# Weighing before copying: the order of two readers of one PSUM bank in a four-layer network

## The chip, the cores and the metric

The kernel is one launch on one core of a Trainium2 chip. The metric is the device time of a whole execution in microseconds; lower is better. All arithmetic is in float32.

## The reference, cut to what matters

The input is 4 images of 32 x 32 tokens with 384 channels. Four residual layers follow each other; the change lies in layer 1, an attention with 12 heads of width 32 whose weights are multiplied by a "group weight":

```python
sim = sigmoid(beta + alpha * einsum('bhnd,bhmd->bhnm', l2norm(xg_h), l2norm(gc)))   # n = 1024, m = 256
group_weight = einsum('bhnm,bhkm->bhnk', sim, sim)                                   # n x n, symmetric
gamma = sigmoid(group_gamma)
group_weight = group_weight * gamma + (1.0 - gamma)
attn = softmax(einsum('bhnd,bhmd->bhnm', q, k) * scale, axis=-1)
attn = attn * group_weight
attn = attn / (attn.sum(axis=2, keepdims=True) + 1e-08)
out = einsum('bhnm,bhmd->bhnd', attn, v)
```

Layer 0 is a deformable attention with a gathered bias, layer 2 a box filter, layer 3 an outlook attention; they are untouched.

## The kernel before

The four images are worked in two lanes. The *front* computes layer 0 of an image; the *trunk* computes layers 1 to 3. While the trunk works on image b, the front's generator is advanced for image b + 1, so that both lanes' instructions are recorded interleaved; for the last image the trunk is alone. A scheduler then puts each engine's instructions in an order by priorities and by its own estimates, places the tiles and sets the semaphores. So a change in one place of the source can move instructions of either lane on every engine, and the order is fixed when the program is built.

Layer 1 works in six *pairs* of heads (`pair`, p = 0 to 5). In a pair, r = 0, 1 names the head. The 1024 x 1024 matrices are worked in eight steps j = 0 to 7 of 128 rows, and each step in two halves h = 0, 1 of 512 columns. A step does this:

- L1443: GpSimd scales the step's 128 columns of `sim` into `sg` (by gamma and a constant).
- L1460: TensorE makes the logits of both heads in a two-bank tile `big`, with 64 rows of the array for each head; L1468: ScalarE takes the exponential into `e`. A tile `big` exists twice.
- For each half h and head r, TensorE makes 128 x 512 group weights in one PSUM bank `ps`. The matrix is symmetric: blocks already computed in an earlier step are transposed from a kept copy (L1485), the others are made by matmuls of `sg` and `sim` (L1490).
- L1498: where the bank holds blocks that a later step needs, ScalarE copies them to `keep` (tiles `gn` and `gf`; 1 to 4 blocks of 128 columns). This is so for 480 of the 768 banks.
- L1499: VectorE *weighs*: it adds 1 - gamma to the bank, multiplies by `e` in place, and leaves the row sums in `tot`.
- After the halves of h = 0, `sums_step` prepares the next pair's softmax sums: L1333 makes logits (four matmuls, on 32 rows of the array each) in two `big` tiles, L1341 (VectorE) takes their maximum and L1342 (ScalarE) the exponential in place, with its sum.
- `values` of the step before: L1423 to L1426 (VectorE) make reciprocal sums and scale the values, and L1432 (TensorE) multiplies them with `e` into the bank `av`.

In step 6 `sums_finish` turns the next pair's sums into logarithms by small operations (L1359 to L1365 on VectorE, L1362 on ScalarE), L1367 transposes them on TensorE, L1370 stores them and `load_lse` (L1309) loads them as an additional row of the queries; L1303 loads queries and keys. In the last step `sims` (L1380, L1388, L1391) computes the next pair's `sim`.

There are four single PSUM banks (`bank`) in rotation for everything, one of them taken by `av` through a pair. The front takes its own from the same four: L820 (attention logits), L833 (transposes of a running maximum, made by L826 on VectorE), L841 (broadcast by a matmul, after L839 on GpSimd), L855 (attention values). The front's other operations named later are L799 (gathers, GpSimd's queue), L811 and L816 (ScalarE) and L812 and L817 (VectorE), which interpolate the bias, and L853 (ScalarE's exponential).

Two readers of one bank never overlap: the semaphores let them follow each other as the source has them. Where there is a copy, the weighing of L1499 waits for it, and TensorE may write the bank again after both.

## Time and profile before

| What | us |
|---|---|
| Median of 3 runs | 4660.67 (4658.08 to 4672.65) |
| The profiled execution | 4698.26, span 4696.5 |
| TensorE busy in the span | 4148.5 |
| VectorE busy | 3181.2 |
| ScalarE busy | 2293.4 |
| GpSimd busy | 948.8 |
| L1499, weighing: 768 of 749 ns | 562.4 |
| L1498, copies: 192 of 583 ns (`gf`); 96 each of 475, 369 and 263 ns (`gn`) | 106.3; 45.1, 35.4 and 25.2 |
| L1490, group weights on TensorE | 865.1 |

PE is TensorE, PEld its weight loads, DVE VectorE, ACT ScalarE, POOL GpSimd and SP the queue that issues most DMAs. Busy times overlap and do not add up to the span. In a list of waits, "A <- B: t, n, m" says that A's engine sat idle for t us in all, n times, at most m us, until B was done. In the timeline a bracket gives the idle time ahead of an instruction and what ended it.

### The profile page before, as it was taken

The numbers are of one execution on the slowest core, as the hardware profiler recorded it, in microseconds if no ns is written. First come the engines' busy times: TensorE is split into PE (matmuls) and PEld (weight loads), VectorE is DVE, ScalarE is ACT, GpSimd is POOL, SyncE is SP. The second block draws the span as 40 slices with busy tenths as digits, with TensorE's granted clock in tenths as the row PEclk, the third lists the DMA queues.
The fourth block names the chain that finished last, engine by engine and source line by source line (L and its number), as shares of the span: only waits on it lengthen the run. The fifth ranks groups of instructions, "written<-read, shape, count | busy, mean of one in ns | idle before, by whom it ended". The sixth has DMA issues, their size and how long they took to land. (4 is left out here: it accounts for less than half of the span.)

```text
span 4696.5 us, 46832 instructions
## 1 busy us (share of the span) xinstructions
PE 4148.5 (88%) x15704; PEld 1782.4 (38%) x15704; DVE 3181.2 (68%) x6005; ACT 2293.4 (49%) x3631; POOL 948.8 (20%) x946
## 2 busy tenths in 40 slices
PE   5477797999999988999999989899999998999998
PEld 2222243333333353433333444333333345343444
DVE  3599755787868726677877763768787884565654
ACT  2166433566656313456665432446565651455532
POOL 0533204221212103311211110422021211000000
PEclk8688898999999988999999989899999998999998
DMA  6435234322212144321211124531121213311011
GB/s 124 132 112 152 65 103 131 90 62 55 71 33 70 58 139 131 114 62 51 82 51 56 58 79 116 161 91 53 37 78 51 75 37 115 108 31 27 19 40 41
DMA packets 232819, 370.98 MB, mean 79 GB/s; under 512 B 117732, under 2 KB 165697, under 8 KB 232577
## 3 DMA queue, kind: packets, MB, share of 16 engines
q1 hardware_dynamic: 171560, 201.49, 14.7%
q0 software_dynamic: 39936, 145.53, 10.6%
q10 hardware_dynamic: 21080, 20.96, 1.8%
q8 instruction: 124, 2.03, 0.2%
q14 instruction: 119, 0.97, 0.1%
HBM read 287.90 MB, written 80.27 MB: 78 GB/s over the span
## 5 line engine op out<-in xcount | busy, mean ns | idle before, releaser
L1490 PE MATMUL bank<-whole,sg 128*128 128x512 f32 (+3 forms) x2304 | 865.1, 510 | 8.3 <-POOL sg L1443 6.9
L1499 DVE SCALAR_TENSOR_TENSOR e<-bank,gam,e 128x512 f32<-128x512 f32 x768 | 562.4, 749 | 445.9 <-ACT gn L1498 159.6
L1342 ACT ACTIVATE big<-big,nmax 128x1024 f32<-128x1024 f32 x384 | 418.5, 1090 | 353.5 <-DVE nmax L1341 338.0
L1468 ACT ACTIVATE e<-big 128x1024 f32<-128x1024 f32 x384 | 379.5, 1018 | 412.2 <-PE big L1460 406.3
L1490 PEld LDWEIGHTS bank<-whole,sg 128*128 128x128 f32 x2304 | 407.4, 199 | 376.6 <-issue 286.5
L1341 DVE TENSOR_REDUCE nmax<-big 128x1 f32<-128x1024 f32 x384 | 454.8, 1220 | 70.0 <-PE big L1333 38.7
L799 POOL DMA_INDIRECT win<-strips,widx x288 | 311.5, 1082 | 683.8 <-DVE z L812 408.9
L1443 POOL TENSOR_SCALAR sg<-whole,gam 128x512 f32<-128x512 f32 x192 | 150.3, 785 | 1453.1 <-PE bank L1490 1003.6
L1460 PE MATMUL big<-qa,ka 64*128 64x512 f32 x1536 | 422.4, 622 | 8.2 <-ACT big L1342 7.6
L1333 PE MATMUL big<-k,q 32*128 32x512 f32 x1536 | 328.3, 679 | 77.9 <-ACT e L1468 40.7
L820 PE MATMUL bank<-qpad,kz 128*128 128x512 f32 x576 | 281.8, 617 | 12.4 <-DVE e L1499 12.4
L714 POOL DMA_INDIRECT gat<-pairs,sidx x192 | 206.3, 1075 | 410.9 <-DVE ix_gt L500 223.6
L855 PE MATMUL bank<-lg,va 128*64 128x512 f32 x576 | 266.0, 606 | 15.0 <-ACT lg L853 14.9
L855 PE MATMUL bank<-lg,ones 128*64 128x512 f32 x576 | 265.3, 605 | 0.0
L817 DVE SCALAR_TENSOR_TENSOR lg<-z,bias_f,lg 128x512 f32<-128x512 f32 x288 | 221.1, 776 | 40.2 <-ACT lg L816 39.0
L811 ACT ACTIVATE z<-win,bias_f 128x528 f32<-128x528 f32 x288 | 208.4, 738 | 66.7 <-DVE lg L817 32.3
L1460 PEld LDWEIGHTS big<-qa,ka 64*128 64x128 f32 x1536 | 138.0, 186 | 263.1 <-issue 155.6
L812 DVE SCALAR_TENSOR_TENSOR z<-win,bias_f,z 128x528 f32<-128x528 f32 x288 | 214.6, 763 | 26.3 <-DMA win<-strips,widx 16.8
L852 DVE TENSOR_TENSOR lg<-lg,tb 128x512 f32<-128x512 f32 x288 | 187.4, 697 | 42.4 <-ACT tb L845 42.4
L1432 PE MATMUL bank<-e,vs 128*32 128x512 f32 x1536 | 206.7, 604 | 1.0 <-DVE vs L1426 1.0
L816 ACT ACTIVATE lg<-z,bias_f 128x512 f32<-128x512 f32 x288 | 200.3, 718 | 13.6 <-PE bank L855 6.7
L821 DVE TENSOR_TENSOR lg<-bank,lg 128x512 f32<-128x512 f32 x288 | 192.2, 685 | 20.2 <-PE bank L820 18.3
(302 smaller groups left out, 6593.9 us busy)
## 6 DMA issues: line engine op xcount, KB each, us to landing
pairs<-xn SPq DMA_DIRECT2D x64, 192.0 KB
q<-qd SPq DMA_DIRECT2D x48, 256.0 KB
w<-in_gmat SPq DMA_DIRECT2D x16, 576.0 KB
w<-in_w_off SPq DMA_DIRECT2D x12, 576.0 KB
w<-in_Wqkv SPq DMA_DIRECT2D x12, 576.0 KB
a<-in_x SPq DMA_DIRECT2D x16, 384.0 KB
x<-a ACTq DMA_DIRECT2D x4, 1536.0 KB
win<-strips,widx POOLq DMA_INDIRECT x384
```

Of the source, the lines that this page charges most:

```text
L799: nc.gpsimd.indirect_dma_start(out=win, out_offset=None, in_=self.strips[:, :], in_offset=bass.IndirectOffsetOnAxis(ap=self.widx[:, q, c : ...
L812: v.scalar_tensor_tensor(z, wv[:, 1 : HH + 1, 0 : HW + 1], sc(0, 1), z, ALU.mult, ALU.add)
L817: v.scalar_tensor_tensor(lg, z[:, :, 1 : HW + 1], sc(0, 0), lg, ALU.mult, ALU.add)
L820: nc.tensor.matmul(ps, kz[:, j * P : (j + 1) * P], both, start=True, stop=True)
L855: nc.tensor.matmul(po[out, :], w, lf, start=j == 0, stop=j == NJ - 1)
L1333: nc.tensor.matmul(ps[r][:, h * 512 : (h + 1) * 512], self.q4[rows, i * P : (i + 1) * P], self.k4[rows, 0:512], start=True, stop=True,)
L1341: v.tensor_reduce(nmax[:, r, i : i + 1], ps[r], AX.X, ALU.max, negate=True)
L1342: nc.scalar.activation(ps[r], ps[r], AF.Exp, bias=nmax[:, r, i : i + 1], accum_out=den[:, r, i : i + 1],)
L1460: nc.tensor.matmul(ps[:, r, :], ka[rows, j * P : (j + 1) * P], qa[rows, cols], start=True, stop=True,)
L1468: nc.scalar.activation(e, ps, AF.Exp)
L1490: nc.tensor.matmul(ps[:, (mid - i0) * P :], sg[:, r, m, :], sim[:, h, r, m, (mid - i0) * P :], start=m == 0, stop=m == 1,)
L1499: v.scalar_tensor_tensor(e[:, r, :], ps, self.gam[:, 1:2], e[:, r, :], ALU.add, ALU.mult, accum_out=tot[:, r, h : h + 1],)
```

## The change

In the loop over the heads r of `pair`, the weighing now stands ahead of the copy in the source. Both read the same bank, so their semaphores turn round: the weighing waits for TensorE, and the copy waits for the weighing. Nothing else is edited. In the changed kernel the weighing is L1497 and the copy L1502.

```diff
                                 start=m == 0,
                                 stop=m == 1,
                             )
-                    if first < i1:
-                        nc.scalar.copy(keep[:, r, :], ps[:, (first - i0) * P :])
                     v.scalar_tensor_tensor(
                         e[:, r, :], ps, self.gam[:, 1:2], e[:, r, :], ALU.add, ALU.mult,
                         accum_out=tot[:, r, h : h + 1],
                     )
+                    if first < i1:
+                        nc.scalar.copy(keep[:, r, :], ps[:, (first - i0) * P :])
```

The scheduler builds another order from this: compared as lists of instructions, the two orders differ in 108 lines of TensorE's 8898 (removed and added ones counted), 806 of VectorE's 5239, 634 of ScalarE's 3325, 68 of SP's 998 and 20 of GpSimd's 951.

## The prediction

> **What bounds the kernel now.** I read the page first, then the busy time by stretch, then the waits of TensorE and VectorE, then the chain of waits and the timeline at the places that these name. The page:

> ```profile
> PE 4148.5 (88%) x15704; PEld 1782.4 (38%) x15704; DVE 3181.2 (68%) x6005; ACT 2293.4 (49%) x3631; POOL 948.8 (20%) x946
> ```

> TensorE has most of the span. The edited instructions live in layer 1's pairs, which run in four stretches: three in which the next image's front shares the engines (784 to 1600, 1990 to 2700, 3090 to 3800 us) and the last image alone (4066 to 4560 us). Busy time in the third and the last (columns: stretch, length, then PE, PEld, DVE, ACT, POOL in us with counts, granted clock, DMA share, GB/s):

> ```profile
> 3090.00:3800.00 710.00, 662.21 (x2621) 268.96 (x2620) 554.04 (x1092) 430.69 (x692) 147.83 (x152) 0.98 0.23 65
> 4066.00:4560.00 494.00, 480.43 (x2131) 207.74 (x2129) 287.67 (x675) 265.19 (x419) 33.96 (x50) 0.99 0.11 28
> ```

> In a shared stretch TensorE idles 710 - 662 = 48 us and VectorE is 78% busy; alone, TensorE idles 14 us of 494. The first two shared stretches leave 53 and 46 us. All idle TensorE time that the edit could touch is thus about 147 + 14 = 161 us, 3.4% of the span. VectorE's largest waits on ScalarE, whole run:

> ```profile
> DVE e L1499 <- ACT gn L1498: 159.6, 163, 4.0
> DVE e L1499 <- ACT gf L1498: 157.9, 101, 2.0
> ```

> Weighings (L1499) stood idle for 317.5 us until the copy (L1498) of the same bank was done. That is the wait which the edit removes; but it is VectorE's, and counts only where TensorE then waits. TensorE's waits in the third stretch:

> ```profile
> PE big L1333 <- ACT e L1468: 13.7, 14, 1.8
> PE bank L1367 <- DVE dsum L1365: 5.5, 5, 1.4
> PE bank L841 <- POOL diag L839: 5.1, 6, 1.0
> PE bank L833 <- DVE rmax L826: 4.6, 7, 1.7
> PE bank L820 <- DVE e L1499: 4.1, 4, 1.6
> PE big L1333 <- ACT big L1342: 4.0, 4, 1.5
> PE bank L855 <- ACT lg L853: 2.4, 3, 1.0
> PE bank L1485 <- DVE e L1499: 2.3, 2, 1.4
> PE big L1380 <- ACT e L1468: 1.8, 2, 1.0
> ```

> VectorE ended 5.5 + 4.6 + 4.1 + 2.3 = 16.5 us, ScalarE 13.7 + 4.0 + 2.4 + 1.8 = 21.9 us. The first sum can shrink, the second can grow.

> [...] a copy starts at 4177.70 and takes 0.27, its weighing starts at 4178.00. [...] in the chain eight 64-row matmuls of L1460, issued together, take 1.92 us, and two that a matmul of L1367 had cut off take 1.73:

> ```profile
> 4174.51 1.92 PE big L1460 x8
> 4221.81 1.73 PE big L1460 x2
> ```

> **The change part by part.** No instruction, byte or DMA is added or removed.

> *The wait removed.* All 480 weighings whose bank is also copied waited for ScalarE. In the changed program they wait for TensorE alone (and for the exponentials, long done). I lined up the 120 copies of the stretch 3000 to 3800 us with their weighings, each put at the later of its bank's last matmul and the end of the VectorE instruction that stands ahead of it in the changed order: 93 start earlier, by 79 us together; in the last image 100 of 120, by 85 us.

> *The wait added.* Each copy now waits for its weighing (749 ns, and 84 ns for the accumulator's read), and behind it in ScalarE's queue wait exponentials and front work. By the same count 51 of 120 copies hold up the next ScalarE instruction, 36 us in that stretch (mostly L853, L811, L816). ScalarE had 710 - 431 = 279 us idle there; its share of the chain of waits in that stretch was 90 of 679 us, 13%. I price the hold-up at that share: 36 x 0.13 = 4.7 us a stretch. From both sides: nothing, if the scheduler's new order hides it, or a third of it (12 us), if it lands on exponentials for which TensorE waits.

> *The order moved.* The scheduler reacts: L1342's second exponential often goes ahead of the first copy, and weighings go ahead of front work (L812, L817) on VectorE. On TensorE 11 of L1460's groups that were split 3 + 1 come together (29 to 18), L1380 loses one split an image, L1333 gains two an image. At 1.73 - 0.96 = 0.77 us a split (0.96 is half of 1.92), a shared stretch gains 2 + 1 - 2 = 1 of them, 0.8 us; the price for the other two lines is unknown and taken as the same (0 to 1.5). On SP's queue the store of lse and its two reloads (L1370, L1309) pass two loads of qa and ka (L1303), which are needed a pair later; on POOL three operations an image trade places with gathers issued many blocks ahead. Both cost nothing while that distance covers them[...].

> *Last image, each pair but the last, at the end of its sums.* The timeline now:

> ```profile
> 4217.52 0.26 ACT L1498 COPY gn<-bank 128x128 f32<-128x128 f32 x1
> 4218.92 0.18 DVE L1359 CAST dsum<-den 128x16 f32<-128x16 int32 x1 [0.35 <-ACT big L1342]
> 4219.07 0.75 DVE L1499 SCALAR_TENSOR_TENSOR e<-bank,gam,e 128x512 f32<-128x512 f32 x1
> 4219.75 0.17 DVE L1360 TENSOR_SCALAR dsum<-dsum 128x16 f32<-128x16 f32 x1
> 4221.53 0.28 PE L1367 MATMUL bank<-ident,dsum 128*16 128x128 f32 x1 [1.27 <-DVE dsum L1365]
> ```

> The second weighing sits inside the chain from L1359 to L1367. In the changed order both weighings run ahead of L1359, at 4217.45 to 4218.9, while ScalarE does its exponentials; L1359 starts as before, three tiny operations take the weighing's place, and two copies (0.26 each) stand before L1362. L1360 ends near 4219.3 in place of 4219.92; I take 0.55 us. L1367 now stands ahead of both matmuls of the second L1460 tile, which saves the split, 0.77. Together 1.3 us for each of 5 pairs: 6.6 us. At a pair's first step the copy (0.49) leaves the path to L1341, but L1333 ends only 0.16 us ahead of it: 0.2 x 5 = 1 us. The other steps gain nothing, TensorE having no gap there. Last image: -7.6 us.

> *A shared stretch.* L1367: 5 x 0.55 = 2.75 us. L833: VectorE is late since two weighings waited behind two exponentials and a copy (3243.8 in place of 3242.1 us); 1.7 us is more than the 0.66 us of each wait, and it is the cause in about 5 of 7: 3 us. L1485: about half, 1 us. L820: nothing, since a bank comes free when both readers are done, whichever is last. Splits 0.8. Sum 7.5, less 4.7: 2.8 us, three times: 8.4 us.

> Total -7.6 - 8.4 = -16 us. The profiled execution took 4698.26 us (span 4696.5), 0.8% over the median of 4660.67, so it would read 4682; the median, 4660.67 - 16 = about 4645 us.

> **The rivals.**
> (a) *VectorE was the late one* (chance 0.20): the whole 16.5 us a stretch goes, as do the diag waits (5.1) behind L833: 3 x 21.6 + 7.6 = 72 us, 4590 us. For it: 79 us of earlier starts on an engine 78% busy. Against: TensorE then meets ScalarE's 21.9 us.
> (b) *The hold-up passes to ScalarE and decides* (0.30): copies sit at the head of ScalarE's queue in the shared stretches until a VectorE with 78% of its time taken serves them, exponentials L1468 come late, and L1333, which waits for their tile (13.7 us already), waits longer. At a third of 36 us with the gains of 7.5 halved: 3 x (12 - 3.8) - 7.6 = +17 us, 4678; with all gains gone, 4689. It decides once more than 7.5 + 2.5 = 10 of the 36 us, 28%, reach TensorE.
> (c) *Nothing in the shared stretches* (0.18): the two waits cancel and only the last image gains: 4653 us, within the noise.
> My forecast itself has 0.32. That the edit does nothing is excluded: the built program shows all 480 waits turned round.

> **How the numbers follow.** A measurement of this kernel can tell about 0.3% (14 us) from no change. Forecast: more than half of the outcomes near -16 are beyond it, so of 0.32 I put 0.23 to faster; (a) adds 0.20: 0.43. Within 0.3%: 0.09 of the forecast, 0.16 of (c), 0.02 of (b): 0.27. Slower: 0.28 of (b), 0.02 of (c): 0.30. The range runs from 4600, most of (a), to 4690, (b) with all gains gone; the forecast's own range is 4630 to 4657.

> **What would show it.** In the changed profile VectorE's waits on copies should be gone, with copies waiting on weighings in their place, some 100 us or more in all. In the last image L1460's second tile should end 1.3 us sooner after L1333 in each pair's step 6 (the wait of L1367 by itself need not shrink, as L1367 now stands a matmul earlier), and the pairs 7 to 8 us sooner. L833's wait should fall from 4.6 to under 2 us a stretch. L1333's wait for L1468 should stay under 18 us a stretch; if it passes 25, (b) is right. Were the last image not shorter, my reading of L1367 would be wrong.

## The result and the profile after

The changed kernel is faster: 4635.8 us median against 4660.67 us in the first measurement, a ratio of 0.9945 (95% interval 0.9928 to 0.9962), 25 us (18 to 34). Two repetitions, e1_after and e3_after below, gave 0.9942 (0.992 to 0.9965) and 0.9918 (0.99 to 0.9937). The profiled execution took 4633.41 us (span 4631.6).

The page after, and the busy time by stretch, in a shared stretch and in the last image (columns as in the prediction; the windows lie where the same work now stands):

```profile
PE 4107.5 (89%) x15704; PEld 1772.9 (38%) x15704; DVE 3182.5 (69%) x6005; ACT 2310.3 (50%) x3631; POOL 948.7 (20%) x946
```

```profile
3035.00:3745.00 710.00, 664.69 (x2623) 270.37 (x2622) 556.70 (x1092) 436.25 (x692) 147.03 (x150) 0.97 0.22 66
4015.00:4496.00 481.00, 470.11 (x2129) 204.57 (x2129) 286.35 (x674) 267.09 (x419) 33.55 (x50) 1.00 0.11 28
```

VectorE's and ScalarE's work is what it was. TensorE now idles 710 - 664.7 = 45 us in the shared stretch (48 before) and 11 us in the last image (14). The last image's window holds the same 2129 to 2131 matmuls in 481 us instead of 494; some 3 us of that difference is clock, by my estimate. The clock records hold only 1.0 and 0.5, in multiples of 3.41 us (see below); I call each 3.41 us a window. Four windows of this stretch were halved in the first profile and one after. In the profiles of the two repetitions e1_before and e1_after none was, and the five pairs take 409.5 and 400.7 us. The first profile's take 414.0, 4.5 us more than e1_before's; shared among its four halved windows this is 1.1 us each, and the estimate is three of them. The waits of VectorE and ScalarE, whole run:

```profile
DVE e L1497 <- PE bank L1490: 219.5, 224, 3.8
...
ACT gn L1502 <- DVE e L1497: 132.4, 121, 4.1
...
DVE e L1497 <- PE bank L1485: 122.7, 51, 5.6
```

The 317.5 us that weighings stood idle for copies are gone, but VectorE's idle time ahead of the weighings falls by less, from 445.9 to 346.0 us in all, since most of it is now a wait for TensorE. Copies now wait for weighings: 132.4 us here and 48.8 for gf, 181 us together. TensorE's waits in the shared stretch (3039 to 3749 us):

```profile
PE big L1333 <- ACT e L1468: 11.2, 10, 2.0
PE bank L1367 <- DVE dsum L1365: 5.6, 5, 1.5
PE big L1333 <- ACT big L1342: 5.0, 5, 1.5
PE bank L833 <- DVE rmax L826: 3.3, 6, 1.8
PE bank L820 <- ACT gf L1502: 3.1, 2, 1.6
PE big L1380 <- ACT e L1468: 2.8, 2, 1.5
PE bank L841 <- POOL diag L839: 2.7, 3, 1.0
PE big L1460 <- ACT big L1342: 2.5, 1, 2.5
...
PE bank L841 <- DMA gc<-gcd: 1.7, 2, 0.8
```

L1333's wait for the exponentials L1468, the place where rival (b) had to show, is 11.2 us instead of 13.7. L820 now waits for a copy where it waited for a weighing, for 3.1 us instead of 4.1. L1367's wait is unchanged. L841's wait for diag is 2.7 us instead of 5.1, but a row of 1.7 us that names a DMA stands beside it now, so that L841 waits 4.4 us in all.

Where the time went shows at two places of each pair. The chain of waits in the last image, end of a pair's sums; before (columns: start, length, what):

```profile
4300.89 1.22 DVE nmax L1341
...
4304.69 0.18 DVE dsum L1359
4304.86 0.74 DVE e L1499 x2
4305.60 0.09 DVE dsum L1360
...
4307.29 0.28 PE bank L1367
4307.57 1.05 PE big L1460 x2
```

and after:

```profile
4239.83 0.24 PE big L1333 x3
...
4242.41 1.42 DVE e L1497 x4
4243.83 0.17 DVE dsum L1359
...
4244.21 0.08 DVE rt L1424
...
4245.81 0.28 PE bank L1367
4246.09 1.06 PE big L1460 x4
```

In this view one weighing is x2, as its record is followed by that of the accumulator's read (0.08 us). The second weighing has left the stretch between L1359 and L1367; both now stand ahead of L1359. The stretch takes 4307.29 - 4304.69 = 2.60 us before, 4245.81 - 4243.83 = 1.98 after. From the end of L1333 to the start of L1367 it is 6.40 us before and 5.74 after. Now a pair's first step, before:

```profile
4157.51 1.09 ACT big L1342
...
4158.64 1.20 ACT big L1342 x2
4159.85 0.48 ACT gf L1498
...
4160.35 0.76 DVE e L1499 x2
4161.11 1.15 DVE nmax L1341
...
4162.35 1.21 ACT big L1342 x2
...
4163.60 1.82 PE big L1460 x5
```

and after:

```profile
4183.55 1.21 ACT big L1342 x2
...
4184.81 1.13 PE big L1333 x4
...
4185.94 1.13 PE big L1333 x4
4187.06 1.91 PE bank L1490 x4
4188.98 1.48 PE big L1460 x5
```

Before, the chain ran through the copy, the weighing, the maximum and the exponentials, and TensorE waited at L1460; from the first L1342 to L1460 it took 6.09 us. After, copy and weighing are off the chain, TensorE's own matmuls are the chain, and it takes 5.43.

**A yardstick free of the clock.** The medians of the kernel before lay between 4660.67 and 4695.83 us in four sessions (the last three on three different chips), and its two profiles have granted clocks of 0.927 and 0.933. The clock records hold only 1.0 and 0.5 (full and half clock), in pieces that are multiples of 3.41 us (but for the last piece, which the record's end cuts): 170 pieces in the first profile before, 146 in the one after. So I took, in each profile, the time from an image's first L1460 to the first L1460 of its sixth pair, times the mean granted clock in it. In the three profiles whose shared stretches are as before this "full-clock length" is 625.9, 626.0 and 625.8 us (mean of three images), in three of the changed kernel 619.4, 620.0 and 619.4. In e1_shared, whose shared stretches have the changed kernel's orders too, it is 617.9. The last image: 407.2 and 409.5 before, 400.6, 400.7 and 400.5 after. The product takes 3.41 x 0.5 = 1.7 us off for a halved window even where TensorE stood idle in part of it: I take this to be why the first profile, with four halved windows there, comes to 407.2 and e1_before, with none, to 409.5. So I read these lengths to about 2 us. The edit is worth some 6.4 us in each shared stretch and some 8 in the last image (8.8 between the two profiles without a halved window): 3 x 6.4 + 8 = 27 us, what the chip's times say.

### The profile page after: what moved, and what is told of

It reads as the page before. It is cut to its first block, busy times and chain, and to the rows that moved or that the text cites. A ratio compares the mean times of both kernels' runs of the same rounds, so it can differ in the third digit from the quotient of the medians.

```text
span 4631.6 us, 46942 instructions
## 1 busy us (share of the span) xinstructions
PE 4107.5 (89%) x15704; PEld 1772.9 (38%) x15704; DVE 3182.5 (69%) x6005; ACT 2310.3 (50%) x3631; POOL 948.7 (20%) x946
## 4 chain that ended last, share of the span: by engine, by line
PE 59%; DVE 19%; ACT 7%; issue 7%; DMA 4%; POOL 3%; ACTq 0%; SPq 0%; DVEq 0%; POOLq 0%
PE bank L1490 13%; PE big L1460 5%; PE big L395 5%; PE big L1333 4%; PE bank L820 4%; PE bank L409 4%; PE bank L855 4%; PE bank L1485 3%; PE bank L1432 3%; DVE nmax L1341 2%; PE big L644 2%; POOL gat L714 2%; DVE e L1497 2%; PE bank L1170 2%; PE big L1615 1%
## 5 line engine op out<-in xcount | busy, mean ns | idle before, releaser
L1490 PE MATMUL bank<-whole,sg 128*128 128x512 f32 (+3 forms) x2304 | 852.1, 504 | 6.9 <-POOL sg L1443 6.9
L1497 DVE SCALAR_TENSOR_TENSOR e<-bank,gam,e 128x512 f32<-128x512 f32 x768 | 561.5, 746 | 346.0 <-PE bank L1490 219.5
L1342 ACT ACTIVATE big<-big,nmax 128x1024 f32<-128x1024 f32 x384 | 417.5, 1087 | 322.4 <-DVE nmax L1341 321.5
L1468 ACT ACTIVATE e<-big 128x1024 f32<-128x1024 f32 x384 | 379.5, 1018 | 360.2 <-PE big L1460 359.3
L1490 PEld LDWEIGHTS bank<-whole,sg 128*128 128x128 f32 x2304 | 404.0, 198 | 367.1 <-issue 280.4
L1341 DVE TENSOR_REDUCE nmax<-big 128x1 f32<-128x1024 f32 x384 | 454.4, 1217 | 79.1 <-PE big L1333 78.4
L1460 PE MATMUL big<-qa,ka 64*128 64x512 f32 x1536 | 413.9, 625 | 8.4 <-ACT big L1342 8.2
L1333 PE MATMUL big<-k,q 32*128 32x512 f32 x1536 | 328.8, 678 | 78.2 <-ACT big L1342 43.1
L820 PE MATMUL bank<-qpad,kz 128*128 128x512 f32 x576 | 281.7, 618 | 9.4 <-ACT gf L1502 9.4
L855 PE MATMUL bank<-lg,va 128*64 128x512 f32 x576 | 265.7, 605 | 15.0 <-ACT lg L853 14.9
L855 PE MATMUL bank<-lg,ones 128*64 128x512 f32 x576 | 265.0, 605 | 0.0
L817 DVE SCALAR_TENSOR_TENSOR lg<-z,bias_f,lg 128x512 f32<-128x512 f32 x288 | 214.5, 761 | 47.4 <-ACT lg L816 45.9
L811 ACT ACTIVATE z<-win,bias_f 128x528 f32<-128x528 f32 x288 | 203.0, 735 | 56.9 <-DVE lg L817 35.2
L1460 PEld LDWEIGHTS big<-qa,ka 64*128 64x128 f32 x1536 | 134.6, 186 | 252.7 <-issue 122.7
L812 DVE SCALAR_TENSOR_TENSOR z<-win,bias_f,z 128x528 f32<-128x528 f32 x288 | 215.3, 771 | 11.3 <-ACT z L811 10.2
L1432 PE MATMUL bank<-e,vs 128*32 128x512 f32 x1536 | 206.7, 604 | 3.6 <-DVE vs L1426 3.6
L816 ACT ACTIVATE lg<-z,bias_f 128x512 f32<-128x512 f32 x288 | 200.0, 716 | 12.3 <-PE bank L855 6.4
```

Of the source, the lines that this page charges most:

```text
L820: nc.tensor.matmul(ps, kz[:, j * P : (j + 1) * P], both, start=True, stop=True)
L855: nc.tensor.matmul(po[out, :], w, lf, start=j == 0, stop=j == NJ - 1)
L1333: nc.tensor.matmul(ps[r][:, h * 512 : (h + 1) * 512], self.q4[rows, i * P : (i + 1) * P], self.k4[rows, 0:512], start=True, stop=True,)
L1341: v.tensor_reduce(nmax[:, r, i : i + 1], ps[r], AX.X, ALU.max, negate=True)
L1342: nc.scalar.activation(ps[r], ps[r], AF.Exp, bias=nmax[:, r, i : i + 1], accum_out=den[:, r, i : i + 1],)
L1432: nc.tensor.matmul(av[r0 : r0 + HD1, :], vs[:, r, :], es[h][:, r, :], start=j == 0, stop=j == NJ - 1,)
```

## The experiments

All results in one table: us are the ratio's distance from 1 times the median of before in the same session (4690.65 for e1, 4695.83 for e2 and 4684.69 for e3). "Half clock" is the time that the profile's whole span lost to lowered clock, span x (1 - clock).

| Run | Ratio (95%) | us | Full-clock length, shared / last | Half clock |
|---|---|---|---|---|
| before, first profile | | | 625.9 / 407.2 | 343 |
| e1_before | 1.001 (0.9995 to 1.0024) | +5 | 626.0 / 409.5 | 312 |
| e1_after | 0.9942 (0.992 to 0.9965) | -27 | 620.0 / 400.7 | 312 |
| e1_last | 0.9982 (0.997 to 0.9995) | -8 | 625.8 / 400.3 | 338 |
| e1_shared | 0.995 (0.993 to 0.997) | -23 | 617.9 / 408.9 | 324 |
| e2_step6 | 0.9971 (0.9958 to 0.9985) | -14 | 624.6 / 403.6 | 307 |
| e2_step0 | 1.001 (0.9991 to 1.0028) | +5 | 624.4 / 403.9 | 351 |
| e2_others | 0.9951 (0.9928 to 0.9973) | -23 | 622.9 / 408.4 | 305 |
| e2_uncoupled | 0.9904 (0.9878 to 0.9931) | -45 | 616.3 / 401.3 | 322 |
| e3_after | 0.9918 (0.99 to 0.9937) | -38 | 619.4 / 400.5 | 317 |
| e3_twice | 1.0014 (0.9999 to 1.0028) | +7 | 623.3 / 400.9 | 357 |
| e3_not0 | 0.9927 (0.9909 to 0.9944) | -34 | 618.8 / 401.6 | 328 |
| e3_late | 0.9924 (0.9902 to 0.9945) | -36 | 620.8 / 400.7 | 299 |

### Which images gain

Both kernels once more (no edit), and the swap in the last image alone or in the first three alone. The edit of all kernels that swap in part of the places is this, with another condition:

```diff
-                    if first < i1:
+                    swap = self.b == NB - 1
+                    if first < i1 and not swap:
                         nc.scalar.copy(keep[:, r, :], ps[:, (first - i0) * P :])
                     v.scalar_tensor_tensor(
...
+                    if first < i1 and swap:
+                        nc.scalar.copy(keep[:, r, :], ps[:, (first - i0) * P :])
```

**e1_before:**

> The kernel before once more, unchanged, as the yardstick for the profiled steps: 0 against itself, within about 10 us. If the 25 us between the two kernels are partly clock, the pairs of this profile should be shorter than the 81.5 to 85.1 us of the first profile's last image (about 80.8 each).

**e1_after:**

> The changed kernel once more. Theory (a gain of about 0.75 us at step 0 and again at step 7 of nearly every pair but the last of an image): -15 to -30 us against before. Rival (only the last image gains, the rest of the difference was the clock): -8 us.

**e1_last** (`swap = self.b == NB - 1`, with `self.b = b` set as each image begins):

> Copy behind the weighing in the last image alone. My theory: 5 pairs x (0.78 at step 0 + 0.75 at step 7) = -8 us. Rival (the gain is all in the shared stretches): 0.

**e1_shared** (`swap = self.b < NB - 1`):

> Copy behind the weighing in the first three images alone. My theory: TensorE's fixed gaps at steps 0 and 7 shrink there too where the front does not fill them, -3 to -6 us an image, -9 to -18 us in all. Rival (front work fills those gaps and copies hold up ScalarE): 0 to +10 us.

The pairs of e1_before's last image took 81.8 to 82.1 us without a halved window, not 80.8, and those of e1_after 80.0 to 80.3: the clock is not what made the two kernels differ there. Last image alone: -8 us (-14 to -2), the full-clock length 400.3 as in the changed kernel, and 625.8 in the other three as before. Shared images alone: -23 us (-33 to -14), beyond what I had expected, with 408.9 left in the last image. The two parts add up to the whole within the intervals. So some 20 us of the gain come from the shared stretches, where the prediction had put 8.

### Which steps gain

**e2_step6** (`swap = j == NJ - 2`):

> The swap only in step 6 of each pair, where the chain of L1359 to L1367 stands. My theory: the second weighing leaves that chain and TensorE's gap shrinks by 0.75 us in each of the last image's five pairs and in three of five pairs of each shared image, 14 x 0.75 = -10.5 us. Rival (the shared images gain by the order of front work, not by this chain): the last image alone, -3.8 us.

**e2_step0** (`swap = j == 0`):

> The swap only in step 0 of each pair. My prediction priced it at 0.2 a pair, -1 us; what the trace of the changed kernel suggests is 0.78 for each of five pairs of the last image, -4 us, and little more in the shared images. Rival (half of the shared images' gain comes from here, as front work follows these copies): -12 us.

**e2_others** (`swap = 0 < j < NJ - 2 or j == NJ - 1`):

> The swap in all steps but 0 and 6. My theory: no gap of TensorE in the last image, 0 there; in the shared images L833's wait (about 4.3 to 1.7 us) and that for diag (3.3 to 0.9 us) go with these steps, -5 us each, -15 us in all. Rival (those waits go with steps 0 and 6): 0.

I compared the starts of L1460 step by step in the trace. In e2_step6 the time around L1367 is 0.75 us shorter in all five pairs of the last image and in three of five in each shared one, and no other step of the last image gains. In e2_step0 the first step is 0.78 us shorter in four of the five pairs of the last image and the second by 0.27. In that image all four engines that compute run their instructions in the same order as before, so the turned waits alone do this. In e2_others no step of the last image gains; in the shared images the fifth step is 0.43 us shorter in most pairs, and L833's wait is down from 4.2 to 1.0 us a stretch. The wait of L841 did not behave as expected: it is 2.5 us instead of 3.3 in e2_others and in e2_step6 alike (there as 0.8 for diag and 1.7 in the row of the DMA). At full clock the three parts are worth 1.4, 1.6 and 3.1 us a shared stretch, 6.1 together, against 6.4 for the whole; each of the first two is too small for these lengths to show by itself.

e2_step6 measures -14 us (-20 to -7) where -10.5 was expected. The times of the other two do not follow their parts: e2_step0 gains 3 x 1.6 + 4.5 = 9 us at full clock and measures +5 (-4 to +13), e2_others 3 x 3.1 = 9 and measures -23 (-34 to -13). The half clock of their profiles has the signs of the differences: 351 us in e2_step0, 305 in e2_others. It is so in all their executions, each of which has its granted clock on record: on average 341 us in e2_step0 (14 executions) and 309 in e2_others (7), against 333 in the kernel before beside them (36). From one execution of a kernel to another, 1 us more at half clock goes with some 0.7 us more time (0.72 over the 247 executions of the experiments). At that rate the clock accounts for most of e2_others' gain, some 17 us for the 24 by which its average is lower, and in e2_step0 it takes back some 6 us for 8; these are estimates. A window of e2_step0's last image and the two after it (columns as before; the clock is the third number from the end):

```profile
4389.52:4392.93 3.41, 2.13 (x6) 0.48 (x5) 1.61 (x11) 1.60 (x4) 0.00 (x0) 1.00 0.28 70
4392.93:4396.34 3.41, 3.41 (x12) 2.27 (x14) 1.52 (x4) 1.02 (x1) 0.00 (x0) 0.50 0.46 120
4396.34:4399.76 3.42, 3.42 (x24) 2.19 (x22) 1.77 (x4) 2.30 (x2) 0.00 (x0) 1.00 0.00 0
```

TensorE was idle for 1.28 us ahead of L1367 in the first window; in the next its clock was 0.50 for the whole 3.41 us. That is 1.7 us at half clock, some 1.2 us of time by the rate of 0.7, more than the 0.78 that the pair had gained. How often a halved window follows such a one is counted below.

### What the copies' waiting costs

**e2_uncoupled** (against the kernel before):

```diff
-                    if first < i1:
-                        nc.scalar.copy(keep[:, r, :], ps[:, (first - i0) * P :])
...
+                    if first < i1:
+                        nc.scalar.copy(keep[:, r, :], sim[:, h, r, 0, (first - i0) * P :])
```

> The weighing as in the changed kernel, and the copy takes its 128 columns from sim in SBUF and not from the bank, so that neither waits for the other; what the copies hold is then not the group weights. My prediction's hold-up of ScalarE (4.7 us a shared stretch): 3 x 4.7 = 14 us less than the changed kernel, -41 us against before. Rival (nobody pays for the copies' waiting): as the changed kernel, -27 us.

-45 us (-57 to -32), where -41 was the value for a hold-up as priced in the prediction; the interval touches that of the changed kernel. At full clock a shared stretch takes 616.3 us against 619.6: 3.3 us less, so some 3 us is about the most that the copies' waiting costs. The traces show it at the banks, which come free earlier since the copy no longer reads them: in the five pairs of a shared stretch TensorE's wait at L820 is 1.2 us instead of 3.1, at L1485 0.2 instead of 1.0. L1333's wait for the exponentials L1468, where a held-up ScalarE had to show, is not shorter (13.7 us against 11.9). Other waits move both ways (L1490's of 2.3 us is gone, L833's is 3.6 instead of 1.7), as ScalarE and VectorE run in another order here, so what the queue alone costs is not shown.

**e3_after:**

> The changed kernel, as the yardstick of this group: -27 us against before, as in its first repetition, give or take 10.

-38 us, 11 more than in the first repetition. In its six executions half clock took 312 us on average, in the 19 of the kernel before beside them 326; in the first repetition it was 322 and 323.

**e3_twice** (against the changed kernel):

```diff
                     if first < i1:
                         nc.scalar.copy(keep[:, r, :], ps[:, (first - i0) * P :])
+                        nc.scalar.copy(keep[:, r, :], ps[:, (first - i0) * P :])
```

> The changed kernel with each of its 480 copies issued twice, so that ScalarE's queue is held for some 150 us more, about as much as the 181 us of the copies' waiting. Theory (the waiting of the copies is nearly free, ScalarE has room where TensorE looks to it): within 6 us of the changed kernel. My prediction's price (13% of ScalarE's time in the three shared stretches, some 110 of the 150 us, reach TensorE): +14 us. Rival (b) of the prediction, at a third: +37 us.

My theory of that moment fell: the second copy costs 4692.25 - 4651.79 = 40 us, near the figure for rival (b). The profile tells in what form. Busy time in the third stretch's five pairs, of e1_after and then of e3_twice:

```profile
3017.40:3659.20 641.80, 599.52 (x2343) 243.23 (x2343) 493.49 (x950) 390.56 (x623) 128.49 (x130) 0.96 0.23 64
```

```profile
3039.20:3690.10 650.90, 604.86 (x2343) 244.23 (x2342) 494.73 (x950) 427.71 (x723) 129.96 (x131) 0.96 0.22 63
```

ScalarE has 427.7 - 390.6 = 37 us more to do. At full clock the stretch is 623.3 against 619.4 (e3_after): 3.9 us, 10% of the 37, near the 13% that I used. But the way was another one: the second copy reads the bank too and so frees it later. In the five pairs of a shared stretch L820's wait for the copy is 5.1 us instead of 3.1 and L1485's wait 1.5 instead of 1.1, together about the 2.4 us by which TensorE idles longer, and L1333's wait for L1468 is not longer (11.2 and 11.7). A longer ScalarE queue with the banks free as before was not tried. Over the whole kernel the full-clock lengths give 3 x 3.9 + 0.4 = 12 us; by my estimate most of the other 28 is the clock: 349 us lost at half clock instead of 312, on average over the executions of the two, is some 26 us at the rate of 0.7.

### Two more orders

**e3_not0** (`swap = j > 0`):

> The swap in all steps but 0. Theory (the parts add): step 6's -14 and the others' -23, so -30 to -37 us against before, if step 0 really gives nothing; with step 0's 0.78 x 5 lost, as the changed kernel's -27 + 4 = -23 us.

**e3_late** (against the changed kernel):

```diff
+                banks = []
                 for r in range(2):
...
-                    if first < i1:
-                        nc.scalar.copy(keep[:, r, :], ps[:, (first - i0) * P :])
+                    banks.append(ps)
+                if first < i1:
+                    for r in range(2):
+                        nc.scalar.copy(keep[:, r, :], banks[r][:, (first - i0) * P :])
```

> Both copies of a head's step stand behind both weighings, so that the second weighing never stands behind a copy and the copies wait longer. Theory (banks are free only when both readers are done, and now both are done later): no gain over the changed kernel, -15 to -27 us against before. Rival (VectorE's queue is what counts, and the copies are free): 3 to 8 us faster than the changed kernel.

Neither beats the changed kernel: -34 and -36 us against -38 in the same session, with wide overlaps. e3_late's full-clock lengths (620.8 and 400.7) are within about 1 us of the changed kernel's: once the weighing stands first, the copy's place behind it hardly matters. In e3_not0's trace the first step of each pair of the last image is 0.8 to 1.75 us longer than in e1_after; halved windows, four in that image against none, make up part of it.

## Why the prediction was right, point by point

**Direction and size.** Forecast -16 us (range 4600 to 4690), measured -25 (-34 to -18). The last image was right in its sum, the shared stretches were set too low.

**The waits turned round**, as stated: no weighing waits for a copy, and copies wait 181 us ("some 100 us or more").

**Last image, -7.6 predicted, -8 measured (8.8 in the traces), by wrong terms.** That the sum came out is luck: one term was too large and another too small by about as much. The three terms:
- The chain from L1359 to L1367: 0.55 a pair in the prediction, 0.62 to 0.75 in the traces. Mechanism and size were right.
- The split of L1460's second tile: 0.77 in the prediction, nothing in fact. The step that failed is the price from `4221.81 1.73 PE big L1460 x2`. That pair of matmuls ran at half clock from 4222.05 us on; the windows of the kernel before show it:

```profile
4218.63:4222.05 3.42, 2.15 (x8) 0.75 (x5) 2.17 (x12) 1.96 (x7) 0.00 (x0) 1.00 0.46 123
4222.05:4225.46 3.41, 3.41 (x12) 1.67 (x10) 0.76 (x2) 1.07 (x2) 0.00 (x0) 0.50 0.28 82
```

At full clock the chains above have 1.05 us for the x2 before and 1.06 for the x4 after. A matmul has two records here, so x2 is one head's and x4 both heads', which run side by side on 64 rows of the array each (their records start within 0.01 us). After L1367 the tile thus ends equally late whether one or both are left, and the matmul that ran ahead of L1367 before had only filled a part of TensorE's wait. So L1460's second tile ended 0.75 us sooner and not the 1.3 that the prediction promised as a sign.
- Step 0: 0.2 in the prediction, 0.78 in fact, and 0.27 more in the step behind it. The prediction looked at the step's first group of sums, behind the copy of 0.49 us; there L1341 in fact starts only 0.06 us sooner in the step. The gain is at the step's second group, which the prediction left out: the copy gf and its weighing stood ahead of L1341 (4159.85 to 4161.11 above), L1341 started 1.1 us after its tile was done, and TensorE waited 0.66 us at L1460 for the exponential behind it. In the changed kernel that wait is gone: TensorE's own L1333, L1490 and L1460 follow each other.

**Shared stretches, -2.8 each predicted, -6.4 measured at full clock.** Gross the prediction had 7.5 and a hold-up of 4.7. The uncoupled kernel has 626.0 - 616.3 = 9.7 gross, and about 3.3 are given back by the copies' waiting. So the gain was set 2 us too low and the hold-up some 1.4 too high. Term by term, in the five pairs of a shared stretch (means of the three stretches, of two profiles before and three after): TensorE's idle time falls from 46.7 to 43.0 us, and the rest of the gain is busy time.
- L833 was right: 3 us predicted, 4.3 to 1.7 measured (3.3 in the longer window above, where I had promised under 2).
- L820 was set at nothing and gave 1.0 (4.1 to 3.1). L841, which stands behind L833, was left to rival (a) and gave 1.0 (3.6 to 2.6). These two are about the size of what was missing.
- L1367 and the splits, 2.75 + 0.8 = 3.5 predicted: at full clock L1460's busy time falls from 85.7 to 83.7 us and L1380's from 22.1 to 20.9, since their tiles are split less often, while L1367's own wait is 5.6 instead of 5.1. The two new splits of L1333, which the prediction charged in full, do not show in its busy time (63.2 and 62.8).
- L1485's 1 us did not come (2.3 and 2.2 in the longer windows).
- The hold-up did not show where rival (b) looked for it, at L1333. Some time is given back at L1432, which now waits 1.2 us for VectorE's L1426 and is busy 1.1 us longer.

In these stretches the edit turned the waits and moved the order of the work together. No run holds one fixed there, so what each is worth by itself stays open.

**Rival (b)** needed 28% of the hold-up to reach TensorE. The doubled copies show 10% of ScalarE's added time at full clock, and L1333's wait for L1468 fell, so it was false here. In time, though, those copies cost 40 us for some 110 us of ScalarE's time added in the shared stretches, 36%, which is above its point: the banks and the clock made work on ScalarE as dear as (b) had said, by another way.

**Rival (a)**, VectorE as the late engine (-72 us): L820 kept 3.1 of its 4.1 us, now behind the copy, and L1367 5.6 us of wait, which the prediction had said need not shrink. **Rival (c)**, nothing in the shared stretches, is refuted by e1_shared.

**What the prediction had no term for** is the lowered clock that follows some of the gaps. All 14 traces hold only 1.0 and 0.5, in multiples of 3.41 us, and the two windows shown above with 2.13 us busy and 1.28 idle (e2_step0) and 2.15 busy and 1.27 idle (before) each stand right ahead of one at 0.50. Between before and after, the clock adds little: averaged over the executions half clock was 323 and 322 us in the first repetition, 326 and 312 in the second, and the full-clock lengths alone make the 27 us. For e2_step0, e2_others and e3_twice it is most of the difference between length and time, as estimated from the averages over their executions; no run set the clock by itself. Why these three fall to the sides they do stays open.

## What to carry to other kernels

Where two engines read one PSUM bank, put the reader first on which the longer chain hangs, then ask what the second one holds up: here the first reader's gain was 9.7 us a stretch and the second's waiting cost about 3.3 at most, and what of it the traces show is at the banks that it frees later, though both counts of waiting time were far larger. Before calling a wait gone, add up all rows of the instruction that waited, for a row can come back under another name. Before taking a duration as a price, look at the granted clock in its window, for a row measured at half clock made a gain that wasn't there. And compare lengths times clock next to times: they agreed to about 2 us where the medians moved by 35 from session to session.

## What the runs showed of the hardware

The same gap can have a halved window behind it or none. In the first profile before, TensorE idles 1.24 to 1.28 us ahead of L1367 in each of the last image's five pairs; halved windows follow behind that at 4221.53 us (from 4222.05 on, shown above), none behind the other four. After, the five gaps there are 1.33 to 1.36 us, and none has one behind it. In another execution of the changed kernel (e3_after) three halved windows of the last image lie at 4042.87, 4124.79 and 4206.71 us, 81.92 us or 24 windows apart. A pair of 80.0 us and the 1.7 us of a halved window come near that distance; that the next gap then falls on the same part of a window, and that this is why the clock is halved again, is my guess and was not shown.
